# First FFN of a four-module kernel: the scan's preparation in single parts, two W_dt products to a pair of PSUM banks, light parts at the coming inputs' places

## Chip, cores and metric

The kernel runs on one core of a Trainium2 chip. The metric is the device time of one execution in microseconds (us), the median of several. A measurement of this kernel carries an uncertainty of about 0.2% (3.9 us).

## The reference, cut to what matters

The model is four modules in a row, each behind a layer norm and added to a residual stream x of four batches with 512 tokens and 512 channels: an attention, a first FFN with ternary weights, a selective scan (state space), and a block of latent attention with a mixture of experts. The change lies in the first FFN and in the preparation of the scan:

```python
# first FFN
h1 = jnp.einsum('bsd,hd->bsh', x, w1q)
h3 = jnp.einsum('bsd,hd->bsh', x, w3q)
g = jax.nn.silu(h1) * h3
return jnp.einsum('bsh,dh->bsd', g, w2q)
...
# scan
xz = jnp.einsum('btd,rd->btr', x, W_xproj)
delta_r, B_mat, C_mat = xz[..., :r], xz[..., r:r + n], xz[..., r + n:]
delta = jax.nn.softplus(jnp.einsum('btr,dr->btd', delta_r, W_dt) + b_dt)
dA = jnp.exp(delta[..., None] * A)
Bu = delta[..., None] * B_mat[:, :, None, :] * x[..., None]
h = dA_t * h + Bu_t            # over the tokens t
y = jnp.sum(h * C_t[:, None, :], axis=-1)
```

The hidden width of the FFN is 1365, that of the scan's state is 16, the rank of W_dt is 128. All is float32.

## The kernel before, in words

All four batches' x stay on the chip (xs, one tile each). The modules follow each other; TensorE's order is written by hand in all that matters here (`manual_schedule` for PE: the order of the Python calls is the order of TensorE's queue), while a planner orders the other engines' queues by its own costs. Every engine works through its queue in order.

**First FFN** (lines 676 to 718). The outer loop runs over the four batches b, the inner over eleven pieces f of the hidden width (ten of 128 rows, one of 85). `gated` (646) makes eight products with w1 and eight with w3 into the two halves of a pair of PSUM banks (pg; each product in two parts, high and low, for accuracy), ScalarE applies silu (658), VectorE multiplies by the other half (659, written to the tile sil), and the result is split into gh (ScalarE, 664) and gl (VectorE, 665). `down` (668) multiplies an earlier piece (the one before, for b > 0) by w2 into four single banks. PSUM has eight banks: two pairs (tag pair) and four single ones (tag bank). At the end of a batch VectorE adds the four banks to x (716).

Into this loop two generators are woven, each cut into parts by its yields. `part(n)` is called three times per piece, with n = 3f in the middle of `gated`, 3f+1 behind it, 3f+2 behind `down`: 33 places, n = 0 to 32.

- `inputs(b + 1)` (613), called `coming`: layer norm of the next batch and its transposes (tpf, 635), which ScalarE and VectorE read into hTh (640) and hTl (641). It gets the places n = 14, 17, 20, 23, 26, 29 and 32.
- `prepare(b - 1, ...)` (495), called `between`: all that the scan needs of the batch before. It gets the other places but 2, 3 and 5.

The parts of `prepare` before the change, in order: layer norm; two rows; four times a transpose into uT (131, 132); delta_r (pd, 522) in two parts; B and C (pb, 531) in two parts; B's transpose (pbt, 542); four parts with one W_dt product each (pz, 553), which ScalarE reads for |z + b| (Abs, 554) and VectorE for max(z + b, 0) (555); Exp over the whole tile (557); two parts with two u each (three VectorE operations per u, 561 to 563: the rounding of 1 + e is kept apart); Ln (566) with finish(0) and finish(1); and four parts turn_out(k), the first two with finish(k + 2). `finish` (569) adds Ln's result to delta (570), stores delta to HBM and multiplies it by uT (ux, 573). `turn_out` (575) transposes ux (tpd, 578), ScalarE copies it to the one buffer st (580), and a DMA stores it to dxs. These are 23 parts, and with the coming inputs there are 23 places for them: 0, 1, 4, 6 to 13, 15, 16, 18, 19, 21, 22, 24, 25, 27, 28, 30, 31. In the last pass (b = 3) nothing is coming, there are 30 places and the parts end at place 25.

Each part of `prepare` that needs TensorE takes a half of a pair of banks through `half_pair` (592), and the other half of that pair stays empty.

**Scan** (818 to 969). Eight single banks. For each batch, 16 states n and two halves, a step: ScalarE scales the rows bu (842) and makes da (848), TensorE transposes bu into two banks (856), VectorE scans them (864, 128x512, twice a step), GpSimd multiplies by C (hc, 875), TensorE adds hc up (888). The last batch's `prepare(3)` runs here, with banks of its own through `bank`: seven parts ahead of the steps, one part behind every second step from step 1 on. At step 6 of a batch (`fetch`, 829) the next one's delta_l and dxT, 1 MB each, are loaded; SP's queue issues these loads, the rows of C (cb, 872, one per two steps, into three buffers) and the stores of deltas and dxs. Behind the first batch's scan VectorE normalises it for the next module (`enter`, 107, 108, 738), into memory that held the tiles of `prepare(3)`.

The lines that call it:

```python
def part(n):
    if n % 3 == 2 and n > 3 * 4 and b + 1 < B:
        next(coming, None)
    elif n not in (2, 3, 5):
        next(between, None)
...
between = prepare(b - 1, bs, half_pair, 2) if b > 0 else iter(())
...
between = prepare(B - 1, cp, bank, 4)
```

Of the kernel before, what the change touches and what calls it, by code (L numbers as in the profile page):

```python
# [14 lines left out]
AF = mybir.ActivationFunctionType  # L15
ALU = mybir.AluOpType
# [3 lines left out]
P = 128  # L20
B, T, C = 4, 512, 512
NT = T // P
NK = C // P
# [23 lines left out]
def block_kernel(ctx: ExitStack, tc: tile.TileContext, a: dict, out: bass.AP):  # L47
    nc = tc.nc
# [15 lines left out]
    def pair(name):  # L64
        return banks["pair"].tile([P, 2, 512], F32, tag="pair", name=name)

    def bank(name):
        return banks["bank"].tile([P, 512], F32, tag="bank", name=name)
# [3 lines left out]
    def by_tokens(x, b):  # L72
        return x[b * T : (b + 1) * T, :].rearrange("(t p) c -> p t c", p=P)
# [53 lines left out]
    def transpose_into(dst, src, at, scale=1.0, spot=None):  # L127

        tp = (spot or bank)("tp")
        for k in range(NK):  # L130
            nc.tensor.transpose(tp[:, k * P : (k + 1) * P], src[:, k * P : (k + 1) * P], ident)  # L131
        nc.scalar.activation(  # L132
            dst[:, :, at : at + P], tp.rearrange("p (k q) -> p k q", k=NK), AF.Copy, scale=scale
        )
# [16 lines left out]
    with tc.tile_pool(name="a_w", bufs=1) as aw, tc.tile_pool(name="a_1", bufs=1) as a1, tc.tile_pool(  # L151
        name="a_2", bufs=2
# [234 lines left out]
        with tc.manual_schedule(engines={mybir.EngineType.PE}):  # L387
# [39 lines left out]
            for b in range(B):  # L427
                between = {m: [] for m in range(18)}
# [3 lines left out]
                if b + 1 < B:  # L432
                    n = b + 1
# [39 lines left out]
    wdt = sw.tile([P, C], F32, tag="wdt", name="wdt")  # L473
    nc.sync.dma_start(wdt, a["wdtT"])
    bdt = sw.tile([P, NK], F32, tag="bdt", name="bdt")
# [16 lines left out]
            nc.tensor.matmul(dp[:, k * P : (k + 1) * P], ones, diag, start=True, stop=True)  # L492
        nc.scalar.copy(dpar, dp)

    def prepare(b, pool, spot, ahead):


        x = xs[b]
        uT = pool.tile([P, NK, T], F32, tag="uT", name="uT")
        ops, rows = [], {}  # L500
        layer_norm(pool, x, lambda t, op: ops.append(op))
        yield

        def make(t):
            row = rows[t] = pool.tile([P, C], F32, tag="row", name="row_s", bufs=ahead)
            ops[t](row)
            ud = pool.tile([P, C], F32, tag="u", name="ud")
            nc.gpsimd.tensor_tensor(ud, row, dpar, ALU.mult)
            nc.gpsimd.tensor_tensor(x[:, t, :], x[:, t, :], ud, ALU.add)

        make(0)
        make(1)
        yield
        for t in range(NT):
            transpose_into(uT, rows.pop(t), t * P, spot=spot)
            if t == 1:
                make(2)
                make(3)
            yield
        pd = spot("pd")  # L520
        for k in range(NK):
            nc.tensor.matmul(pd, wx[:, k, :RANK], uT[:, k, :], start=k == 0, stop=k == NK - 1)
            if k == 1:
                yield
        drT = pool.tile([P, T], F32, tag="drT", name="drT")
        nc.scalar.copy(drT, pd)
        yield

        pb = spot("pb")
        for k in range(NK):  # L530
            nc.tensor.matmul(
                pb[: 2 * NS, :], wx[:, k, RANK:], uT[:, k, :], start=k == 0, stop=k == NK - 1
            )
            if k == 1:
                yield
        bcT = pool.tile([2 * NS, T], F32, tag="bcT", name="bcT")
        nc.scalar.copy(bcT, pb[: 2 * NS, :])
        nc.sync.dma_start(c_rows[b], bcT[NS:, :])
        yield
        pb = spot("pbt")  # L540
        for t in range(NT):
            nc.tensor.transpose(
                pb[:, t * NS : (t + 1) * NS], bcT[:NS, t * P : (t + 1) * P], ident[:NS, :NS]
            )
        nc.scalar.copy(bts[:, b, :], pb[:, : NT * NS])
        yield


        delta = pool.tile([P, NK, T], F32, tag="delta", name="delta")
        e = pool.tile([P, NK, T], F32, tag="e", name="e")  # L550
        for k in range(NK):
            pz = spot("pz")
            nc.tensor.matmul(pz, wdt[:, k * P : (k + 1) * P], drT, start=True, stop=True)
            nc.scalar.activation(e[:, k, :], pz, AF.Abs, bias=bdt[:, k : k + 1])
            nc.vector.tensor_scalar(delta[:, k, :], pz, bdt[:, k : k + 1], 0.0, ALU.add, ALU.max)
            yield
        nc.scalar.activation(e, e, AF.Exp, scale=-1.0)
        yield
        for k in range(NK):
            u = pool.tile([P, T], F32, tag="u", name="u")  # L560
            nc.vector.tensor_scalar(u, e[:, k, :], 1.0, -1.0, ALU.add, ALU.add)
            nc.vector.tensor_tensor(u, e[:, k, :], u, ALU.subtract)
            nc.vector.tensor_tensor(delta[:, k, :], delta[:, k, :], u, ALU.add)
            if k % 2 == 1:
                yield
        nc.scalar.activation(e, e, AF.Ln, bias=1.0)
        scaled = {}

        def finish(k):
            nc.vector.tensor_tensor(delta[:, k, :], delta[:, k, :], e[:, k, :], ALU.add)  # L570
            nc.sync.dma_start(deltas[b, k * P : (k + 1) * P, :], delta[:, k, :])
            scaled[k] = pool.tile([P, T], F32, tag="ux", name="ux", bufs=2)
            nc.vector.tensor_tensor(scaled[k], delta[:, k, :], uT[:, k, :], ALU.mult)

        def turn_out(k):
            tp, ux = spot("tpd"), scaled.pop(k)
            for t in range(NT):
                nc.tensor.transpose(tp[:, t * P : (t + 1) * P], ux[:, t * P : (t + 1) * P], ident)
            st = pool.tile([P, NT, P], F32, tag="st", name="st")
            nc.scalar.copy(st.rearrange("p t q -> p (t q)"), tp)  # L580
            nc.sync.dma_start(by_tokens(dxs, b)[:, :, k * P : (k + 1) * P], st)

        finish(0)
        finish(1)
        yield
        for k in range(NK):
            turn_out(k)
            if k + 2 < NK:
                finish(k + 2)
            yield  # L590

    def half_pair(name):
        return pair(name)[:, 0, :]


    with tc.tile_pool(name="b_s", bufs=1) as bs, tc.tile_pool(name="b_1", bufs=1) as b1, tc.tile_pool(
        name="b_2", bufs=2
# [78 lines left out]
        with tc.manual_schedule(engines={mybir.EngineType.PE}):  # L676
            for _ in inputs(0, first_mv):
                pass
            for f in range(3):
                quantize_down(f)  # L680
            for b in range(B):
                hT = high_low.pop(b)
                between = prepare(b - 1, bs, half_pair, 2) if b > 0 else iter(())
                coming = inputs(b + 1) if b + 1 < B else iter(())
                ys = None

                def part(n):  # L690
                    if n % 3 == 2 and n > 3 * 4 and b + 1 < B:
                        next(coming, None)
                    elif n not in (2, 3, 5):
                        next(between, None)


                lag = GBUFS - 1 if b == 0 else 1
                pending = []
                for f, rows in enumerate(FROWS):
                    pending.append((f, rows, gated(b, f, rows, hT, lambda: part(3 * f))))  # L700
                    if b == 0 and f + 3 < NF:
                        quantize_down(f + 3)
                    if b == 0 and f == 6:
                        clear()
                    part(3 * f + 1)
                    if b == 0 and f == 4:
                        scan_constants(b2)
                    if len(pending) > lag:
                        if ys is None:
                            ys = [bank(f"y{t}") for t in range(NT)]  # L710
                        down(b, *pending.pop(0), ys)
                    part(3 * f + 2)
                for job in pending:
                    down(b, *job, ys)
                for t in range(NT):
                    nc.vector.scalar_tensor_tensor(  # L716
                        xs[b][:, t, :], ys[t], scales["w2"][:, 2:3], xs[b][:, t, :], ALU.mult, ALU.add
                    )
# [100 lines left out]
    with tc.tile_pool(name="c_f", bufs=2, reuse_waits="tile") as cf, tc.tile_pool(  # L819
        name="c_1", bufs=1  # L820
# [76 lines left out]
        fetch(0)  # L897
        last = ExitStack()
        cp = last.enter_context(tc.tile_pool(name="c_p", bufs=1, side="right", reuse_waits="tile"))
        between = prepare(B - 1, cp, bank, 4)  # L900
        come = enter(0, c1)
        with tc.manual_schedule(engines={mybir.EngineType.PE}):
            for _ in range(2):
# [124 lines left out]
    with tc.tile_pool(name="d_1", bufs=1) as d1, tc.tile_pool(name="d_2", bufs=2) as d2, tc.tile_pool(  # L1028
        name="d_3", bufs=3
# [145 lines left out]
        with tc.manual_schedule(engines={mybir.EngineType.PE}):  # L1175
# [3 lines left out]
            n = len(pairs)  # L1179
            each = n // B  # L1180
            for m in range(n + 3):
                b, at = divmod(m, each)
# [35 lines left out]
    with tc.tile_pool(name="e_1", bufs=1, reuse_waits="tile") as e1, tc.tile_pool(  # L1218
        name="e_2", bufs=2, reuse_waits="tile"
# [127 lines left out]
        for c in range(2):  # L1347
# [19 lines left out]
            for n in range(TT):  # L1367
                nc.tensor.matmul(
                    found[:, : 2 * n_tiles], unit[:, n, :], what[:, n].rearrange("p s i -> p (s i)"),
                    start=n + c == 0, stop=n + c == TT,  # L1370
# [92 lines left out]
        for t in range(NT):  # L1463
            n = (B - 1) * NT + t
# [74 lines left out]
```

## Time and profile before

| | |
|---|---|
| median of three runs | 1933.17 us (1933.12 to 1936.76) |
| the profiled execution | 1941.33 us |
| its span, first to last instruction | 1939.6 us |
| mean granted TensorE clock | 0.967 |
| busy, share of the span: TensorE, VectorE, ScalarE, GpSimd | 91%, 59%, 49%, 30% |
| first FFN | 433 to 768 us |
| scan | from the first scan operation at 784 us to 1140 us |

The profile is one execution. Rows of a timeline give the start (us from the span's start), the duration (us), engine, line, operation, output <- inputs, shape, how many alike follow each other (xN), and in brackets the idle time of the engine just before with what ended it. A product in full float32 shows as two records. Rows of stages give busy time of each engine in a stretch, with the clock that TensorE was granted (1.00 is full). One execution lasts longer than the median of the unprofiled ones by 8.16 us.

### The profile page before, as it was taken

Reading aid. Unit: us, or ns where it says so; the run is one execution under the profiler, and the core shown is the slowest. Engines: PE = TensorE matmul, PEld = TensorE weight load, DVE = VectorE, ACT = ScalarE, POOL = GpSimd, SP = SyncE. Lnnn points to the kernel's source line nnn. Section 1 sums busy time; section 2 is a strip of 40 time slices with the busy share of each in tenths; the row PEclk is TensorE's granted clock in tenths of the full one; section 3 lists DMA queues with packets and bytes.
Section 4 is the critical chain, followed back from the end, with each engine's and each line's share of the span. In section 5 each row is a group of like instructions: output and inputs, shape, how many; then the busy total and the mean of one; then the engine's idle time right before and its main releaser. Section 6 shows DMA issues by size and latency. Waiting matters only on the chain. (4 is left out here: it accounts for less than half of the span.)

```text
span 1939.6 us, 26716 instructions
## 1 busy us (share of the span) xinstructions
PE 1764.7 (91%) x9970; PEld 1063.5 (55%) x9970; DVE 1143.7 (59%) x1849; ACT 946.0 (49%) x1945; POOL 580.8 (30%) x391
## 2 busy tenths in 40 slices
PE   7999999989999996977888788999999989999998
PEld 3433343437666664766776655555555554544544
DVE  6456435666454545898999985566574663422222
ACT  2433433332242434978999955556675662111111
POOL 2221212120202020966999850000001000144441
PEclk9999999999999998978999987999999999999999
DMA  7003200101000104115131100000001004645445
GB/s 246 8 1 94 75 1 1 44 25 53 1 34 12 44 1 146 40 60 168 53 101 53 50 14 1 1 1 23 1 23 33 23 2 145 223 88 92 87 83 140
DMA packets 67525, 111.09 MB, mean 57 GB/s; under 512 B 7627, under 2 KB 26443, under 8 KB 67349
## 3 DMA queue, kind: packets, MB, share of 16 engines
q1 hardware_dynamic: 58164, 88.02, 13.8%
q0 software_dynamic: 8656, 20.32, 5.8%
q8 instruction: 80, 1.31, 0.3%
q10 hardware_dynamic: 576, 1.05, 0.1%
q14 instruction: 49, 0.39, 0.1%
HBM read 81.18 MB, written 31.33 MB: 58 GB/s over the span
## 5 line engine op out<-in xcount | busy, mean ns | idle before, releaser
L875 POOL TENSOR_TENSOR hc<-h,cb 128x1024 f32<-128x1024 f32 x128 | 303.4, 2415 | 43.5 <-DVE h L864 28.9
L864 DVE TENSOR_TENSOR_SCAN h<-da,bu 128x512 f32<-128x512 f32 x256 | 289.5, 1197 | 19.4 <-ACT da L848 12.2
L856 PE MATMUL bu<-ident,bu 128*128 128x128 f32 x1024 | 163.7, 291 | 48.8 <-DVE h L864 25.0
L271 PE MATMUL pq<-wqkv,hT 128*128 128x512 f32 x384 | 180.9, 619 | 0.7 <-ACT hT L132 0.7
L842 ACT ACTIVATE bu<-dxT,bts 128x512 f32<-128x512 f32 x256 | 164.4, 721 | 4.6 <-DVE x L716 2.8
L856 PEld LDWEIGHTS bu<-ident,bu 128*128 128x128 f32 x1024 | 122.7, 148 | 79.9 <-ACT bu L842 42.9
L848 ACT ACTIVATE da<-delta_l,am 128x511 f32<-128x511 f32 x256 | 164.6, 721 | 3.6 <-DVE h L864 3.6
L1116 ACT ACTIVATE pr<-scd,nm 128x128 f32<-128x128 f32 (+3 forms) x256 | 132.9, 527 | 58.8 <-DVE nm L1113 56.0
L888 PE MATMUL ys<-ident,hc 128*128 128x128 f32 x1024 | 144.4, 286 | 16.0 <-POOL hc L875 14.0
L653 PE MATMUL pg<-hTh,w 128*128 128x512 f32 (+1 forms) x352 | 148.6, 422 | 4.1 <-DVE sil L659 2.9
L653 PE MATMUL pg<-hTl,w 128*128 128x512 f32 (+1 forms) x352 | 141.5, 402 | 0.2 <-DVE hTl L641 0.2
L1418 PE MATMUL pgr<-wgu,gTe 128*128 x304 | 137.1, 593 | 0.0
L888 PEld LDWEIGHTS ys<-ident,hc 128*128 128x128 f32 x1024 | 121.6, 148 | 26.7 <-POOL hc L875 23.4
L351 ACT ACTIVATE pt<-sc 128x1024 f32<-128x1024 f32 (+3 forms) x128 | 84.1, 697 | 84.2 <-PE sc L346 81.7
L271 PEld LDWEIGHTS pq<-wqkv,hT 128*128 128x128 f32 x384 | 72.0, 196 | 94.7 <-issue 86.2
L1105 PE MATMUL scd<-qkTd 32*128 32x512 f32 (+3 forms) x512 | 108.3, 504 | 12.9 <-ACT pr L1116 11.9
L102 POOL TENSOR_TENSOR ri_ln<-ri_ln,minus_half 128x4 f32<-128x4 f32 (+1 forms) x17 | 16.9, 993 | 319.0 <-DVE ri_ln L101 314.5
L1113 DVE TENSOR_REDUCE nm<-scd 128x2 f32<-128x256 f32 (+3 forms) x128 | 104.0, 813 | 0.0
L1128 PEld LDWEIGHTS tpd<-ident,pr 128*128 128x128 f32 x640 | 70.5, 145 | 60.9 <-issue 41.2
L1128 PE MATMUL tpd<-ident,pr 128*128 128x128 f32 x640 | 102.3, 292 | 0.6 <-ACT pr L1116 0.6
L352 POOL TENSOR_SCALAR_AFFINE_SELECT pt<-pt 128x512 f32<-128x512 f32 x64 | 43.1, 674 | 196.7 <-ACT pt L351 196.7
L1108 DVE TENSOR_TENSOR scd<-scd,neg 128x256 f32<-128x256 f32 x128 | 54.7, 428 | 66.7 <-PE scd L1105 64.9
(263 smaller groups left out, 3107.8 us busy)
## 6 DMA issues: line engine op xcount, KB each, us to landing
cb<-c_rows SPq DMA_DIRECT2D x64, 256.0 KB, 3.1
q_w<-in_w2T SPq DMA_DIRECT2D x20, 256.0 KB, 2.9
deltas<-delta SPq DMA_DIRECT2D x16, 256.0 KB, 2.6
dxs<-st SPq DMA_DIRECT2D x16, 256.0 KB, 2.3
delta_l<-deltas SPq DMA_DIRECT2D x4, 1024.0 KB, 9.5
dxT<-dxs SPq DMA_DIRECT2D x4, 1024.0 KB, 7.1
hrows<-h SPq DMA_DIRECT2D x4, 1024.0 KB, 5.4
acc<-x SPq DMA_DIRECT2D x16, 256.0 KB, 2.0
```

The source lines that it names most:

```text
L271: nc.tensor.matmul(y, inputs_T[b][:, k, t * P : (t + 1) * P], wqkv[:, k, s * C : (s + 1) * C], start=k == 0, stop=k == NK - 1,)
L653: nc.tensor.matmul(pg[:rows, i, :], w[:, k, f * P : f * P + rows], part[:, k, :], start=k + m == 0, stop=k + m == NK,)
L842: nc.scalar.activation(row, dxT[:, t, :], AF.Copy, scale=bts[:, b, t * NS + n : t * NS + n + 1])
L848: nc.scalar.activation(da[:, k, 1:], delta[:, k, 1:], AF.Exp, scale=am[:, k, n : n + 1])
L856: nc.tensor.transpose(bu[i][:, t * P : (t + 1) * P], scaled[b, n][t][:, k * P : (k + 1) * P], ident)
L864: nc.vector.tensor_tensor_scan(h[:, i, :], decays[b, n][:, 2 * half + i, :], bu, 0.0, ALU.mult, ALU.add)
L875: nc.gpsimd.tensor_tensor(hc, states.pop((b, n, half)), weighed[b, n].unsqueeze(1).to_broadcast([P, 2, T]), ALU.mult)
L888: nc.tensor.matmul(sums[b][t][:, k * P : (k + 1) * P], hc[:, i, t * P : (t + 1) * P], ident, is_transpose=True, start=n == 0 and k == 0, s ...
L1105: nc.tensor.matmul(sc[:, i, :w], qkT[at, g, t * P : w], qkT[at, NG + g, :w], start=True, stop=True)
L1116: nc.scalar.activation(pr[:, i, :w], sc[:, i, :w], AF.Exp, bias=nm[:, i : i + 1], accum_out=sums[b, g][:, t, 2 * p + i : 2 * p + i + 1],)
L1128: nc.tensor.transpose(tp[:, j * P : (j + 1) * P], pr[:, i, j * P : (j + 1) * P], ident)
L1418: nc.tensor.matmul(pg, gT[:, k, :], wgu[:, bass.ds(e, 1), k, :].rearrange("p e o -> p (e o)"), start=k == 0, stop=k == NK - 1,)
```

## The change

It touches `prepare`, the function that hands out PSUM, and `part`; the arithmetic stays the same.

- `prepare` gets a second argument for PSUM, `spots`, which gives two spots at once: in the FFN the two halves of one pair of banks (`halves`), in the scan two single banks. The four W_dt products are made two by two, in two parts in place of four.
- The parts behind them are cut smaller: each u is a part, Ln is a part, finish(0) and finish(1) are parts, and each finish(k + 2) is a part behind its turn_out. `prepare` has 27 parts in place of 23.
- A yield tells whether the coming part needs no TensorE (True: Exp, u, Ln, finish). At a place that goes to the coming inputs, `part` lets such a light part go along.

The parts' places in the passes b = 1 and 2 are then: W_dt products at 15 and 16, Exp at 17, u at 18 to 21, Ln at 22, finish(0) and finish(1) at 23 and 24, turn_out at 25, 27, 30 and 31, finish(2) and finish(3) at 26 and 28. In b = 3: W_dt products at 14 and 15, Exp 16, u 17 to 20, Ln 21, finish 22 and 23, turn_out 24, 26, 28 and 29. In the scan the W_dt products come behind the steps 9 and 11 (before: 9, 11, 13, 15) and the turn_outs behind the steps 29, 33, 37 and 39 (before: 25, 27, 29, 31).

```diff
-    def prepare(b, pool, spot, ahead):
+    def prepare(b, pool, spot, spots, ahead):
...
-        for k in range(NK):
-            pz = spot("pz")
-            nc.tensor.matmul(pz, wdt[:, k * P : (k + 1) * P], drT, start=True, stop=True)
-            nc.scalar.activation(e[:, k, :], pz, AF.Abs, bias=bdt[:, k : k + 1])
-            nc.vector.tensor_scalar(delta[:, k, :], pz, bdt[:, k : k + 1], 0.0, ALU.add, ALU.max)
-            yield
+        for half in range(2):
+            for i, pz in enumerate(spots("pz")):
+                k = 2 * half + i
+                nc.tensor.matmul(pz, wdt[:, k * P : (k + 1) * P], drT, start=True, stop=True)
+                nc.scalar.activation(e[:, k, :], pz, AF.Abs, bias=bdt[:, k : k + 1])
+                nc.vector.tensor_scalar(delta[:, k, :], pz, bdt[:, k : k + 1], 0.0, ALU.add, ALU.max)
+            yield half == 1
         nc.scalar.activation(e, e, AF.Exp, scale=-1.0)
-        yield
+        yield True
         for k in range(NK):
...
-            if k % 2 == 1:
-                yield
+            yield True
         nc.scalar.activation(e, e, AF.Ln, bias=1.0)
+        yield True
...
         finish(0)
+        yield True
         finish(1)
         yield
         for k in range(NK):
             turn_out(k)
             if k + 2 < NK:
+                yield True
                 finish(k + 2)
             yield
...
+    def halves(name):
+        both = pair(name)
+        return both[:, 0, :], both[:, 1, :]
...
-                between = prepare(b - 1, bs, half_pair, 2) if b > 0 else iter(())
+                between = prepare(b - 1, bs, half_pair, halves, 2) if b > 0 else iter(())
...
+                light = [False]
                 def part(n):
                     if n % 3 == 2 and n > 3 * 4 and b + 1 < B:
                         next(coming, None)
-                    elif n not in (2, 3, 5):
-                        next(between, None)
+                        if not light[0]:
+                            return
+                    if n not in (2, 3, 5):
+                        light[0] = next(between, False)
...
-        between = prepare(B - 1, cp, bank, 4)
+        between = prepare(B - 1, cp, bank, lambda name: (bank(name), bank(name)), 4)
```

## The prediction

> **What bounds the kernel now.** I read the share of busy time first (TensorE 91% over the span), then the busy time by stage, then each engine's timeline around the changed code, with the idle time in front of each instruction. In the first FFN (433 to 768 us) the stage rows show TensorE busy 63.1 of 70 us in pass b=1, 82.2 of 88 in b=2, 79.3 of 92 in b=3: TensorE sets the stage's end and only its idle time can be won. TensorE's timeline names the large holes. The first row below is a gated product, the other three are turn_out's first transpose in the passes b=1, 2, 3:
>
> ```profile
> 559.43 0.50 PE L653 MATMUL pg<-hTh,w 128*128 128x512 f32 x1 [1.38 <-DVE sil L659]
> ...
> 570.72 0.63 PE L578 MATMUL tpd<-ident,ux 128*128 128x128 f32 x4 [3.15 <-DVE hTl L641]
> ...
> 661.33 1.12 PE L578 MATMUL tpd<-ident,ux 128*128 128x128 f32 x4 [3.06 <-DVE hTl L641]
> ...
> 742.97 1.09 PE L578 MATMUL tpd<-ident,ux 128*128 128x128 f32 x4 [9.13 <-DVE ux L573]
> ```
>
> The transposes wait because Ln, finish(0) and finish(1) stand directly before them and VectorE's queue is full. After each of them the granted clock is halved; after the 1.38 us it isn't. Busy time by window (us; PE, PEld, DVE, ACT, POOL, then clock):
>
> ```profile
> 557.92:561.34 3.42, 2.04 (x10) 1.59 (x9) 3.39 (x7) 1.21 (x2) 0.00 (x0) 1.00 0.00 0
> 571.58:575.00 3.42, 3.42 (x12) 2.68 (x11) 1.39 (x3) 0.87 (x2) 0.00 (x0) 0.50 0.59 211
> 660.33:667.16 6.83, 5.83 (x18) 4.86 (x19) 3.76 (x7) 1.80 (x2) 0.00 (x0) 0.50 0.44 159
> 738.84:745.66 6.82, 2.69 (x9) 2.34 (x10) 4.30 (x7) 2.63 (x3) 0.00 (x0) 0.50 0.31 115
> ```
>
> One W_dt product with its two readers is the row from which the new wait is priced (TensorE, ScalarE, VectorE):
>
> ```profile
> 538.70 1.02 PE L553 MATMUL pz<-drT,wdt 128*128 128x512 f32 x2
> 539.15 0.80 PE L653 MATMUL pg<-hTh,w 128*128 128x512 f32 x1
> ```
> ```profile
> 539.76 0.69 ACT L554 ACTIVATE e<-pz,bdt 128x512 f32<-128x512 f32 x1 [2.93 <-PE pz L553]
> ```
> ```profile
> 540.48 0.75 DVE L555 TENSOR_SCALAR delta<-pz,bdt 128x512 f32<-128x512 f32 x1 [2.93 <-ACT e L554]
> ```
>
> In the scan, prepare(3) runs beside b=0. VectorE is busy 108.4 of 116 us there; its two holes, and one preparation operation that waits for GpSimd to finish an hc (0.69 us elsewhere), are:
>
> ```profile
> 833.33 2.75 DVE L562 TENSOR_TENSOR u<-e,u 128x512 f32<-128x512 f32 x1
> ...
> 892.41 2.33 DVE L864 TENSOR_TENSOR_SCAN h<-da,bu 128x512 f32<-128x512 f32 x2 [5.75 <-ACT da L848]
> ```
> ```profile
> 914.45 1.00 DVE L738 TENSOR_SCALAR h<-x,mv_d,ri_ln 128x512 f32<-128x512 f32 x2 [3.27 <-POOL ri_ln L102]
> ```
>
> **The change, part by part.** The number of instructions stays the same on every engine, and behind the scan the order is the same: all is decided between 538 and about 930 us. The sum is made against the profiled execution, 1941.33 us (span 1939.6); the median of the runs is 1933.17, and I carry the difference over.
>
> *1. What goes.* Exp, the four u parts, Ln and finish(0), finish(1) now come at places 17 to 24 in b=1 and 2 and the first turn_out at 25, where Ln and finish stood at 25 and turn_out at 27 before; the last turn_out keeps its place (31). So the waits ahead of the transposes go, with the half clock behind them. b=1: 1.38 + 3.15, and 1.8 for the half clock (the block of eight gated products took 3.14 us from 571.10 instead of 1.86, transposes and first products some 0.5 more). b=2: 1.38 + 3.06, half clock 2.9 (same way). b=3: 9.13, half clock 1.35 (half of the 2.69 us of work in the window). Sum 6.3 + 7.3 + 10.5 = 24.1 us.
>
> *2. What comes: a wait inside a pair.* In the built program both halves are one tile, and the second W_dt product waits on VectorE: by the semaphore count, for the max of the first half, which waits for its Abs. TensorE's order is written by hand, so the gated products behind it wait too. Price: the first product occupies TensorE 0.86 us (538.70 to 539.79, where the gated products come at their steady 0.23 again, less 0.23). Abs starts 1.06 us after the product, max ends at 541.23 (540.48 + 0.75), and TensorE resumes some 0.07 us later (559.37 to 559.43 elsewhere). 541.30 - 539.56 = 1.74 us idle. Two pairs in each of three passes: 6 x 1.74 = 10.4 us. From below it could be 0, if the wait were covered; but only gated products stand behind, on the same queue. From above, with an Abs or a max (0.69, 0.75) ahead of it, 2.5 each. I take 1.74. Between the pairs eight gated products (1.86 us) cover the second half's readers.
>
> *3. What is late next.* I walk the changed order with these durations (Abs 0.69, table load 1.28, Exp and Ln 1.92, a u part 1.8, max or product with sil 0.75, gl, hTl, ux 0.68). In b=1 and 2 VectorE does u0 and u1 (3.7 us) before the sil product of f=6, so gated 7 waits 0.84; then 0.37 (gated 8), 0.65 (turn_out 0 for ux), 0.83 and 0.38 (turn_out 1 and 2 for hTl): 3.1 each, and up to 0.4 at the end, where st still waits for its predecessor's DMA. In b=3 two table loads and Exp stand ahead of f=5's sil, and u1 ahead of its gl: the down products wait 1.8; turn_out 0 waits 1.08 for f=7's sil product.
>
> b=1: 3.5 + 3.1 + 0.3 - 6.3 = +0.6. b=2: 3.5 + 3.1 + 0.4 - 7.3 = -0.3. b=3: 3.5 + 2.9 - 10.5 = -4.1. **FFN: -4** (-14 without the pair's wait, +6 with waits of 2.5 and a us of each new stall mis-sized).
>
> *4. Half clock behind the new waits.* Between windows with 1.38 us idle (full clock next) and gaps of 3.06 (half clock) nothing in the FFN tells; 1.74 is nearer to 1.38, so I take nothing; the upper end is 2.9 us each, from b=2. The Trainium skill ("TensorE: Matmul & The Clock Gate", Part 1) gives an idle window of about 3.4 us as what halves the clock: by it these waits cost nothing more, but the trace halves it after 3.06 already.
>
> *5. The scan.* There the pair is two banks, two tiles, so no wait within it; the next turn must wait for the scan before it, and VectorE has the two max (1.3 us) to do meanwhile: nothing. The Ln stands where it stood, but u is done earlier. The turn_outs move from steps 25, 27, 29, 31 to 29, 33, 37, 39. That takes st's DMA out of the way of the 1 MB loads of delta_l and dxT, behind which the last one landed late: the 5.75 us go. The 3.27 stay in another form: the next normalisation writes where prepare's tiles lay and waits for all stores of dxs, whose last is now 4 steps (10 us) later; I take 3 again, ends 0 and 6. Against it, u and ux stand apart from each other more, and each start beside an hc may wait the 2.06 of the row above (2.75 - 0.69): one more, ends 0 and 3. Sum -5.75 + 2.06 = **-3.5** (-9 to +4).
>
> Sum: -4 - 3.5 = -7.5: 1933.8 for the profiled execution, **1925.7** for the median.
>
> **Rivals.**
> - *Slower: the half clock.* Each of the six waits is followed by two half-clock windows, as the 3.06 us were: 6 x 2.9 = 17.4, less 7.5: +9.9, **1943**. It decides if a window with about 1.7 us idle counts as idle. For it: 585 to 589 us, where two small gaps (2.03 together) were enough for one window. Against it: 1.38, and that one window each (1.8) would only give +3.3.
> - *No change: the scan gives it back.* The store of st comes last now, VectorE waits for it 6 us, two operations more wait for GpSimd (4.1): scan +4.4, FFN -4: **1933.5**, or up to some us below. For it: VectorE works in order, and the long rows above.
> - *Much faster: the pair's wait doesn't bind.* Without 10.4 us the sum is -17.9: **1915.3**. Only the built order speaks against it. The Trainium skill ("PSUM — Partial Sum Buffer", PSUM bank collisions) keeps engines apart by bank, and the halves are two banks: by it no wait is needed; no run here has shown one.
> - *It doesn't do what it says*: the preparation still ends at place 31, so a part shifted early wins only what the transposes waited; this is in the forecast.
>
> **How the numbers follow.** A measurement of this kernel tells about 0.2% (3.9 us) from no change: 1929.3 to 1937.0. Forecast 0.46 (1921 to 1930), no change 0.24, half clock 0.18, no wait 0.12. Faster: 0.46 + 0.12 = 0.58; same 0.24; slower 0.18. The range leaves out the far parts of the half-clock and the no-wait cases: 1917 to 1941.
>
> **What would show it.** Right: TensorE idle 1.7 us ahead of each second W_dt product in the FFN, released by the max; no wait over 1.2 us at turn_out's first transpose in b=1, 2, 3; the down products of f=5 in b=3 waiting for gl. In the scan: st no longer waiting for its DMA and no 5 us hole before the scans of n=17. Wrong: clock 0.5 right behind the W_dt pairs, a hole of over 5 us at the first normalisation behind b=0's scan, or no idle time within a pair.

## The result, and the profile after

The changed kernel takes 1923.79 us (median of four runs, 1921.02 to 1926.95) beside 1933.97 us for the kernel before (median of four, 1933.12 to 1936.76). The ratio is 0.9945 with a 95% interval of 0.9925 to 0.9966, so it is faster by 0.3 to 0.75%, some 10.6 us of 1935. The forecast was -7.5 us. The profiled execution took 1926.95 us with a span of 1925.2 us, 14.4 us less than that of before. One of the six executions of the kernel e8 below was a slow one of 3411.99 us; it counts in the median given for e8 (1915.92 us, without it 1914.78), but not in its ratio.

TensorE's timeline of the changed kernel, at the places that the prediction spoke of: the two W_dt products of the first pair in b=1, the gated product behind it, and turn_out's first transposes in b=1, 2 and 3.

```profile
540.10 1.02 PE L554 MATMUL pz<-drT,wdt 128*128 128x512 f32 x2
...
542.68 1.12 PE L554 MATMUL pz<-drT,wdt 128*128 128x512 f32 x2 [1.56 <-DVE delta L556]
...
557.80 0.50 PE L660 MATMUL pg<-hTh,w 128*128 128x512 f32 x1 [0.72 <-DVE sil L666]
...
568.43 0.63 PE L579 MATMUL tpd<-ident,ux 128*128 128x128 f32 x4 [0.61 <-DVE ux L574]
...
654.93 0.63 PE L579 MATMUL tpd<-ident,ux 128*128 128x128 f32 x4 [0.61 <-DVE ux L574]
...
738.33 0.66 PE L579 MATMUL tpd<-ident,ux 128*128 128x128 f32 x4 [1.28 <-DVE sil L666]
```

The waits of 3.15, 3.06 and 9.13 us are now 0.61, 0.61 and 1.28; the last is a little over the 1.2 us that the prediction had set as its sign of being right. The new wait stands inside the pair, released by the max (delta). The table of TensorE's waits from 520 to 765 us gives its sum (us in all, times, longest):

```profile
PE pz L554 <- DVE delta L556: 9.4, 6, 1.6
...
PE pg L660 <- DVE sil L666: 1.4, 2, 0.7
PE tpd L579 <- DVE sil L666: 1.3, 1, 1.3
PE tpd L579 <- DVE ux L574: 1.2, 2, 0.6
```

The clock stays full behind the pair and behind the transposes (busy time by window, columns as before; the clock is the 1.00):

```profile
542.80:546.20 3.40, 3.40 (x12) 2.02 (x12) 0.75 (x1) 1.11 (x2) 0.00 (x0) 1.00 0.00 0
...
570.10:573.50 3.40, 3.40 (x19) 2.52 (x18) 3.40 (x6) 1.45 (x3) 0.00 (x0) 1.00 0.78 268
...
656.60:660.00 3.40, 3.40 (x19) 2.52 (x18) 3.05 (x5) 1.45 (x3) 0.00 (x0) 1.00 0.70 242
```

In the scan, VectorE's timeline has no hole of 5.75 us any more. Its cause stood on ScalarE in the kernel before, which had to wait for the store of st before it could copy the next block into it, with bu and da behind:

```profile
888.67 0.58 ACT L580 COPY st<-tpd 128x512 f32<-128x512 f32 x1 [5.00 <-DMA dxs<-st]
```

In the changed kernel the four copies there wait 0.3 us for the store in all. The hole at the first normalisation is still there, and a u operation beside an hc still takes 2.75 us:

```profile
814.87 2.75 DVE L563 TENSOR_TENSOR u<-e,u 128x512 f32<-128x512 f32 x1
...
903.70 1.00 DVE L749 TENSOR_SCALAR h<-x,mv_d,ri_ln 128x512 f32<-128x512 f32 x2 [3.88 <-ACT da L859]
```

By stage, from one x<-y to the next in the FFN, and from the first scan operation to the 225th of 256 (the middle of the last batch):

| us | b=1 | b=2 | b=3 | three passes | scan, 224 operations |
|---|---|---|---|---|---|
| before | 89.25 | 89.36 | 90.21 | 268.8 | 312.3 |
| after | 87.64 | 84.83 | 84.51 | 257.0 | 306.4 |

So this execution won 11.8 us in the FFN where -4 was forecast, and 5.9 us in the scan where -3.5 was forecast. That is 17.7 us, and the span is 14.4 us shorter: the rest of this execution, whose code is as before, took 3.3 us longer.

The scan also shows what the new wait hangs on. The code there has the same order (product, Abs, max, then the second product), but its pair is two single tiles. TensorE makes both products without a wait, as four records in one row:

```profile
797.84 1.88 PE L554 MATMUL pz<-drT,wdt 128*128 128x512 f32 x4
```

In the FFN the two halves are two banks as well, but one tile, and there the second product waits 1.56 us.

### The profile page after: what moved, and what is told of

Read it like the earlier page. It is cut to its first block, busy times and chain, and to the rows that moved or that the text cites. A ratio compares the mean times of both kernels' runs of the same rounds, so it can differ in the third digit from the quotient of the medians.

```text
span 1925.2 us, 26704 instructions
## 1 busy us (share of the span) xinstructions
PE 1756.5 (91%) x9970; PEld 1054.1 (55%) x9970; DVE 1143.7 (59%) x1849; ACT 947.5 (49%) x1945; POOL 581.2 (30%) x391
## 3 DMA queue, kind: packets, MB, share of 16 engines
q10 hardware_dynamic: 576, 1.05, 0.1%
## 5 line engine op out<-in xcount | busy, mean ns | idle before, releaser
L660 PE MATMUL pg<-hTh,w 128*128 128x512 f32 (+1 forms) x352 | 144.7, 411 | 2.4 <-DVE sil L666 1.7
```

The lines of the kernel that those rows point to most:

```text
L660: nc.tensor.matmul(pg[:rows, i, :], w[:, k, f * P : f * P + rows], part[:, k, :], start=k + m == 0, stop=k + m == NK,)
```

## The experiments

All edits are on the changed kernel unless something else is said. Ratios are to the kernel before, run on the same chip; 0.001 is 1.9 us. The kernels of a group (e1 to e4, e5 to e8, e9 and e10) share their runs of the kernel before; across groups, and with the changed kernel's first runs, they are compared by their ratios.

**e1 and e2: each half alone.** In e1 the scan's `prepare(3)` is the function of before (`prepare_old`). e2 is an edit on the kernel before: only the scan's `prepare(3)` is the changed function (`prepare_new`), and the FFN stays as it was.

```diff
# e1, on the changed kernel
-between = prepare(B - 1, cp, bank, lambda name: (bank(name), bank(name)), 4)
+between = prepare_old(B - 1, cp, bank, 4)
# e2, on the kernel before
-between = prepare(B - 1, cp, bank, 4)
+between = prepare_new(B - 1, cp, bank, lambda name: (bank(name), bank(name)), 4)
```

> The FFN keeps the changed preparation, the scan gets the preparation of before. Theory: the two halves of the change add up. The profiled execution after is 11.8 us ahead of before at the end of the FFN, so this kernel gains some 8 us by the median (6 to 12; 1924 to 1928), its FFN passes last 87.7, 84.8 and 84.5 us, and the 5.75 us hole of VectorE and the 3.3 us one in the scan of batch 0 are back. Rival: the scan's holes come from when the FFN ends and not from the places of the turn_outs; then this kernel is as fast as the changed one (within 2 us) and has no 5 us hole.

> The reverse: the FFN of before, the changed preparation in the scan. Theory: 4 us faster than before by the median (2 to 6; 1928 to 1932), the 5.75 us hole ahead of the scans of n=17 gone, a hole of 3 to 4 us ahead of the first normalisation. Rival: the scan gives nothing of its own: within 1.5 us of before.

e1: 1931.4 us, ratio 0.9970 (0.9959 to 0.9980), -5.8 us. e2: 1930.96 us, 0.9974 (0.9961 to 0.9986), -5.0 us. Their sum, -10.8, agrees with the whole, -10.6. The theory of two gains that add up holds, though the FFN's is just below what was expected (6 to 12), and its pass b=2 lasted 87.8 us and not 84.8. VectorE's holes go with the preparation of the scan and not with the FFN's end. e1 has the two of before:

```profile
882.34 2.33 DVE L972 TENSOR_TENSOR_SCAN h<-da,bu 128x512 f32<-128x512 f32 x2 [5.60 <-ACT da L956]
...
904.39 1.00 DVE L846 TENSOR_SCALAR h<-x,mv_d,ri_ln 128x512 f32<-128x512 f32 x2 [3.29 <-POOL ri_ln L102]
```

e2 has only the second, and here the profile names its releaser, the store of st:

```profile
913.25 1.00 DVE L838 TENSOR_SCALAR h<-x,mv_d,ri_ln 128x512 f32<-128x512 f32 x2 [4.04 <-DMA dxs<-st]
```

**e3: pairs only.** The FFN of before with the W_dt products in pairs, and everything behind them in the parts and at the places' rule of before; the scan of before. It is an edit on the kernel before.

```diff
-for k in range(NK):
-    pz = spot("pz")
+for half in range(2):
+    for i, pz in enumerate(spots("pz")):
+        k = 2 * half + i
...
     yield
```

> In the FFN two W_dt products to a pair of banks, but the parts of before behind them (two u each, Ln with finish(0) and finish(1) ahead of the first turn_out) and no light parts at the coming inputs' places; the scan is that of before. Theory: the gain comes from the single parts, the pairs cost. The six waits of 1.57 us are there, the first turn_out still waits (3 us in b=1 and 2, 8 to 9 in b=3) with the half clock behind it: 5 to 10 us slower than before (1938 to 1944). Rival: the pairs win, by putting every later part two places earlier; then it is 4 or more us faster than before.

1942.81 us, ratio 1.0034 (1.0021 to 1.0048): 6.6 us slower than before, as the theory said. The pairs' waits came and the transposes' stayed (TensorE's waits, 520 to 772 us):

```profile
PE pz L554 <- DVE delta L556: 9.4, 6, 1.6
PE tpd L579 <- DVE ux L574: 7.3, 1, 7.3
PE tpd L579 <- DVE hTl L743: 6.2, 2, 3.1
```

Against e1 (same FFN but for the parts, same scan) the single parts with their places are worth 12.4 us, from 1.0034 to 0.9970. The pairs by themselves cost. What they give is two places fewer, which by a count of the places the larger number of single parts needs to fit into the pass; no run had single parts without pairs.

**e4: the products ahead of their readers.**

```diff
-for i, pz in enumerate(spots("pz")):
+pair_z = spots("pz")
+for i, pz in enumerate(pair_z):
     k = 2 * half + i
     nc.tensor.matmul(pz, wdt[:, k * P : (k + 1) * P], drT, start=True, stop=True)
+for i, pz in enumerate(pair_z):
+    k = 2 * half + i
     nc.scalar.activation(e[:, k, :], pz, AF.Abs, bias=bdt[:, k : k + 1])
```

> The changed kernel, but both W_dt products of a pair are issued ahead of the four instructions that read them. Theory: the 9.4 us of idle time within the pairs go; the readers now start behind the second product, so the second pair waits some 0.6 us in each pass: 7.5 us faster than the changed kernel (5 to 9; 1915 to 1919). Rival: the wait only moves, since VectorE and ScalarE get no earlier and the next gated products need what they read: within 2 us of the changed kernel.

1927.6 us, ratio 0.9956 (0.9942 to 0.9969): 2.1 us slower than the changed kernel by the ratios, which their intervals do not tell from none. The rival was right. TensorE's waits from 520 to 765 us show where the saving went:

```profile
PE tpd L582 <- DVE ux L577: 6.8, 3, 2.4
...
PE pz L555 <- DVE delta L559: 3.6, 3, 1.2
```

The pairs' waits fell from 9.4 to 3.6 us, and the first turn_outs' rose from 2.5 to 6.8 (2.19, 2.19 and 2.39). TensorE reaches the transposes earlier, and ux is no earlier: the line W_dt, Exp, u, Ln, ux on ScalarE and VectorE runs from the products to the first turn_out, and it was only 0.6 to 1.3 us longer than the time that TensorE took to get there.

**e5: a longer wait inside the pair.** The max of each pair's first half is done twice in the FFN (the second writes the same values).

```diff
+if ahead == 2 and i == 0:
+    nc.vector.tensor_scalar(delta[:, k, :], pz, bdt[:, k : k + 1], 0.0, ALU.add, ALU.max)
```

> The changed kernel with the max of each pair's first half done twice in the FFN, so that the wait within a pair lasts one more VectorE operation (0.75 us): six waits of 2.3 us in place of 1.57. Theory: the clock is decided in fixed stretches of 3.41 us, and a stretch with about 1.8 us idle or more puts the next one at half clock (1.68 us idle left it at full, 1.99 us halved it in the traces so far). A gap of 2.3 us lies with 1.8 us or more in one stretch in some 60% of the places on that grid: three to five of the six are followed by half clock, 1.7 us each, so 4.5 + 5 to 8 = 9 to 13 us slower than the changed kernel. Rival: the clock falls only where nearly a whole stretch is idle: no half clock behind the pairs, 4.5 us slower.

1933.06 us, ratio 0.9985 (0.9970 to 0.9999): 7.8 us slower than the changed kernel, between the two expectations. Four waits were 2.35 us, two 2.82. Only one of the six was followed by half clock, not three to five. The windows of the clock's own grid say why:

```profile
539.45:542.87 3.42, 1.42 (x5) 0.50 (x3) 1.21 (x2) 0.69 (x1) 0.00 (x0) 1.00 0.00 0
542.87:546.28 3.41, 3.06 (x5) 1.84 (x6) 0.52 (x2) 0.69 (x1) 0.00 (x0) 0.50 0.00 0
...
635.02:638.43 3.41, 1.59 (x5) 1.03 (x6) 1.50 (x2) 0.62 (x2) 0.00 (x0) 1.00 0.00 0
638.43:641.84 3.41, 2.26 (x8) 1.10 (x7) 1.90 (x3) 2.04 (x4) 0.00 (x0) 1.00 0.00 0
```

A window with 2.00 us idle (3.42 less 1.42 busy) put the next at 0.50; one with 1.82 idle left it at 1.00. The other waits lay across a border of the grid, with 1.7 us or less on each side. The theory of a fixed grid holds; my count of how many gaps it would catch was wrong. A wait of 1.57 us never halved the clock in any run.

**e6: the last store from another queue.**

```diff
-nc.sync.dma_start(by_tokens(dxs, b)[:, :, k * P : (k + 1) * P], st)
+queue = nc.scalar if ahead == 4 and k == NK - 1 else nc.sync
+queue.dma_start(by_tokens(dxs, b)[:, :, k * P : (k + 1) * P], st)
```

> The changed kernel, but the last store of dxs in the scan's preparation is issued from ScalarE's queue and not from SP's, where it stands behind the next row of C. Theory: the 3.9 us hole ahead of the first normalisation behind batch 0 is the wait for this store (st is written at 895.5 us, the store is issued at 898.0 and lands some 4 us behind that): it is issued 2.5 us earlier, the hole shrinks to 1 to 1.5 us and the kernel is 2 to 3 us faster than the changed one. Rival: the normalisation waits for ri_ln from GpSimd or for something else: the hole stays between 3 and 4 us and the time within 1 us.

1922.67 us, ratio 0.9929 (0.9910 to 0.9949). In the changed kernel SP's queue shows the store right behind the row of C, 2.5 us after st was written (895.5 us):

```profile
897.62 0.32 SPq L883 DMA_DIRECT2D cb<-c_rows  x1
898.03 0.39 SPq L582 DMA_DIRECT2D dxs<-st  x1
```

In e6 the normalisation follows the scan without a hole (no bracket):

```profile
899.88 4.56 DVE L876 TENSOR_TENSOR_SCAN h<-da,bu 128x512 f32<-128x512 f32 x4
904.35 4.12 DVE L750 TENSOR_SCALAR h<-x,mv_d,ri_ln 128x512 f32<-128x512 f32 x2
```

The hole was the wait for the store: theory right on the cause (the row of the changed kernel, 3.88 us, names ScalarE's da; with the store issued earlier the hole is gone). The scan's 224 operations took 304.0 us instead of 306.4, which is 2.4 us of the 3.88 of the hole. About 0.9 us of what is missing stands in the normalisations: the first two, now beside an hc, take 4.12 us in place of 1.00, and the next two 1.04 in place of 3.26. The difference of 3 us by the ratios is within the two intervals.

**e7: one place earlier.** The preparation also gets place 5, and an empty part holds the first turn_out where it was.

```diff
-    if n not in (2, 3, 5):
+    if n not in (2, 3):
...
         finish(1)
         yield
+        if ahead == 2:
+            yield
```

> The changed kernel; in the FFN the preparation also gets place 5, so its parts stand one place earlier, and an empty part stands ahead of the first turn_out, which keeps its place. The products of a pair are ordered as in the changed kernel. Theory: the line from the W_dt products over Exp, u, Ln and ux is what the first turn_out waits for; with one place more (2.7 us) the waits of 0.61, 0.61 and 1.28 us at its first transpose go, the six waits of 1.57 us stay: 2 to 3 us faster than the changed kernel. Rival: VectorE is behind everywhere and the waits only change their place: within 1 us.

1936.59 us, ratio 1.0002 (0.9989 to 1.0014): 11 us slower than the changed kernel, which neither expectation had. The transposes in b=1 and 2 no longer wait, as the theory said. But Ln, with a table load on either side, now stands ahead of silu in ScalarE's queue:

```profile
560.24 1.28 ACT L566 ACT_TABLE_LOAD   x1 [2.47 <-DVE u L563]
561.53 1.92 ACT L566 ACTIVATE e<-e 128x2048 f32<-128x2048 f32 x1
563.47 1.28 ACT L667 ACT_TABLE_LOAD   x1
564.76 0.69 ACT L667 ACTIVATE sil<-pg,sc_w 128x512 f32<-128x512 f32 x1
```

The gated products wait 3.15 and 3.11 us for sil (1.4 us in all in the changed kernel), and half clock is back behind both. The three passes took 268.2 us. In the changed kernel Ln stands behind that silu. The order on ScalarE is the planner's; that this order alone makes the 11 us was not tried apart.

**e8: e4 and e7 together.**

> Both: the products of a pair ahead of their readers, and the preparation one place earlier with an empty part ahead of the first turn_out. Theory: with the products first alone, 5.8 of the 9.4 us of the pairs' waits were saved but 4.3 came back as waits of the first turn_out for ux; with one place more these have no cause, and the second pair comes two places behind the first: pair waits under 1 us in all, turn_out waits under 1 us each, 7 to 10 us faster than the changed kernel (1914 to 1917). Rival: what is saved ahead of the readers always comes back at the next thing that VectorE makes: within 2 us of the changed kernel.

1915.92 us, ratio 0.9895 (0.9871 to 0.9919): 9.6 us faster than the changed kernel, as the theory said, though neither edit gains alone. TensorE's waits from 512 to 757 us:

```profile
PE pg L665 <- DVE sil L671: 2.3, 2, 1.1
...
PE tpd L582 <- DVE hTl L653: 1.4, 2, 0.7
PE tpd L582 <- DVE sil L671: 1.1, 1, 1.1
```

No row names pz, and TensorE's timeline has no gap of 0.25 us or more ahead of a W_dt product. With the products first the planner leaves Ln behind silu (ScalarE: silu at 557.34, Ln's table load at 558.04), so e7's loss does not come.

**e9 and e10: all three edits, and the changed kernel once more.**

> The three edits together on the changed kernel: products of a pair ahead of their readers, preparation one place earlier with an empty part ahead of the first turn_out, and the last store of dxs from ScalarE's queue. Theory: the gain of the FFN (some 9 us against the changed kernel) and that of the scan (the hole of 3.6 us ahead of the first normalisation gone) are independent and add up: 12 us faster than the changed kernel, ratio to before 0.987 to 0.989. Rival: with the FFN shorter the store is no longer what the normalisation waits for, and the time is that of the two FFN edits alone (0.9895) within 1 us.

> The changed kernel once more, unedited, beside the kernel with three edits on the same chip, with a second profile. Theory: the code of its FFN gave passes of 84.8 us (b=2) in one execution and 87.3 to 87.8 in two others, by where the fixed stretches of the clock fell; the three passes last 257 to 262 us in all, and the ratio to before is 0.9935 to 0.9955. Rival: the first profile shows what this kernel always does: b=2 lasts 84.8 us again, with no half clock in the FFN.

e9: 1914.59 us, ratio 0.9894 (0.9874 to 0.9915). It is the fastest kernel here but not told apart from e8: by the time the rival is right. By the trace the hole ahead of the normalisation is gone and the scan takes 304.0 us instead of e8's 306.2; its FFN took 251.9 us instead of 249.9, with 3.4 us more of half clock at the start of b=2. Whether the store's 2 us are kept in the median stays open.

e10: 1924.48 us, ratio 0.9944 (0.9928 to 0.9960), the same as the first time. Its passes (busy time by window, then the clock):

```profile
499.43:587.86 88.43, 80.46 (x341) 57.35 (x340) 45.91 (x72) 33.69 (x47) 12.66 (x9) 0.99 0.08 25
587.86:675.29 87.43, 82.65 (x341) 59.12 (x341) 45.41 (x69) 33.70 (x47) 12.95 (x9) 0.97 0.08 25
675.29:759.71 84.42, 78.34 (x325) 55.56 (x324) 41.64 (x63) 31.59 (x43) 12.96 (x9) 1.00 0.12 40
```

b=2 took 87.4 us, not 84.8: the theory holds. The same FFN code took 257.0, 259.7 (e1), 261.5 (e6) and 260.3 us (e10), the code of before 268.8 and 268.3 (e2). The means are 259.6 and 268.6, so the FFN's gain is 9.0 us, and 2.8 of the 11.8 in the first profile were the luck of one execution, mostly of where the clock's grid fell.

## Why the prediction was right, point by point

The sign, the likeliest case and the range held; the two parts of the forecast, -4 and -3.5, were each too small in the traces (-9.0 and -5.9). The terms of the FFN, against the first profile (the half clock's trace value is the difference of TensorE's busy time, 243.65 us before and 238.64 after):

| term | forecast, us | trace, us |
|---|---|---|
| 1: waits that go (1.38 and 3.15; 1.38 and 3.06; 9.13) | -18.1 | -18.1 |
| 1: half clock behind them | -6.0 | -5.0 (e1, e6, e10: -1.9 to -2.2) |
| 2: waits inside the pairs | +10.4 | +9.4 |
| 3: what is late next | +9.8 | +5.0 |
| small holes at the passes' ends and starts | not counted | -3.1 |
| sum | -4 | -11.8 |

*1. What goes* was right: every wait named is gone, and the half clock behind it. The half clock that a run keeps behind the end of b=1 (586.67 to 593.5 us in e10) was not in the terms.

*2. The wait inside a pair* was right, in its cause, its releaser and its size: 1.56 us each where 1.74 was worked out. So "the pair's wait doesn't bind" is out for the kernel as it is. But its price was not its length: e4 took away 5.8 us of it and gained nothing that can be measured. The wait overlaps with the line of ScalarE and VectorE that the first turn_out needs anyway; the 9.4 us can only be won together with one place more for this line (e8, -9.6). The case "without 10.4 us the sum is -17.9" therefore counted a saving that by itself comes back, as e4 shows. The Trainium skill ("PSUM — Partial Sum Buffer", PSUM bank collisions), which the prediction cites, finds no need for a wait between two banks. The built program keeps it for the tile that holds both halves: in the scan, where the pair is two tiles, the same order of code makes no wait. Two tiles in the FFN were not tried.

*3. What is late next* is the step that was mis-sized: 5.0 us in place of 9.8. Gated 7 waited 0.72 (0.84 worked out) and the first turn_outs 0.61, 0.61 and 1.28 (0.65, 0.65, 1.08), so these were close. The waits of gated 8 (0.37) and of turn_out 1 and 2 for hTl (0.83 and 0.38) did not come, and the down products of f=5 in b=3 waited 1.1 (0.32 and 0.78) in place of 1.8. In the walk each whole u part went ahead of what stood behind it; VectorE's queue puts hTl and gl between the first and the second of the three operations of u2 (557.66 u, 557.99 hTl, 558.60 gl, 559.19 u). The two holes of 1.05 us in which y waited for gl at the start of b=2 and b=3 went too, which the walk, beginning at the W_dt products, could not see.

*4. No half clock behind the new waits* was right, and the slower rival is out: no window behind any of the 1.57 us waits was halved. The prediction chose the nearer of two values, 1.38 and 3.06 us, and in so far this was luck. Read by the clock's stretches of 3.413 us, the trace of before says more: 1.58 us idle left the next stretch full (732.01 to 735.42 us), 2.06 us halved it (656.92 to 660.33 us). The border can now be drawn in as 1.8 to 2.0 us within one stretch (e5, e2). Even waits of 2.35 and 2.82 us (e5) brought half clock behind one of six and 7.8 us in all, so the rival's 1943 would have needed still longer ones.

*5. The scan.* The 5.75 us went and the hole ahead of the normalisation stayed, 3.88 us where 3 was taken, for the reason given: the last store of dxs (e2 names it, e6 removes it). The "one more" wait for GpSimd did not come: six operations of the preparation are long in both kernels (after: 2.75, 2.75, 2.74, 4.24 for two, and 1.34), and they cost 9.8 us above their usual lengths, as much as before. Without the +2.06 the step would have given -5.6, and -5.9 was measured. (The step's terms as written add up to -3.7, not -3.5.) "The scan gives it back" is out: e2 gains 5.0 us.

*What stays open.* The stages give -9.0 and -5.9, the comparisons of whole runs -5.8 (e1), -5.0 (e2) and -10.6 (whole). The scan's agree; of the FFN's gain about 3 us are missing in the whole runs. What lies outside the three passes and the 224 scan operations took between 853 and 864 us in the twelve profiled executions (858.5 before, 861.8 after, 855.4 in e10), without following the edits, so one profile of each kernel can't place them. Executions of one kernel scatter by 5 us or more (e1: 1927.15 to 1933.16).

## What to carry to other kernels

A wait that a trace shows is worth its length only if the next thing in the queue was ready; before taking one away, follow the line of the other engines from its cause to the next place where they meet, and shorten or shift that line in the same edit (e4 and e7 gain nothing or lose, together they gain 0.5%). Work shifted in single parts pays where it lets short, urgent operations in between; but any part with a table load has to be followed on ScalarE's queue, since a planner may put it ahead of what TensorE waits for. A gain of some microseconds in a stage should be read from two or three executions, since the same FFN code took 257.0 to 261.5 us here.

## What the runs showed of the hardware

The granted clock changes only at the borders of stretches of 3.413 us. In the middle of the FFN's passes, from full clock, the next stretch was halved when about 2.0 us or more of one stretch were idle (1.99 in e2); 1.82 us left it full (e5). The Trainium skill ("TensorE: Matmul & The Clock Gate", Part 1) tells of a window of 3413 ns that runs freely; the trace agrees with 3.413 us. It says that the half clock comes after an idle window of that length; here 2.00 idle of 3.42 was enough, and the measurement decides. Behind the end of pass b=1, 1.40 to 1.44 us of idle time were enough in four executions (before, e1, e2, e7), but 1.62 us left the clock full in the changed kernel's first profile (582.9 to 586.3 us). The products behind that end use 85 of 128 rows. They fill all of the 2.0 us of busy time of that stretch in the kernel before, and 0.07 us of it in the changed one. It may be that such work counts as less than busy. Counted by its rows it would leave 2.1 us idle before and 1.65 after (an estimate), on the two sides of the border above; e1, with 1.70 us by that count, was halved and does not fit, and this was not tried. In the scan, among 128x128 transposes, the idle time alone does not decide: 1.35 us was enough once (e2, at 820.5 to 823.9 us), and 1.95 us left the clock full (e10, at 835.8 to 839.3 us).

A VectorE operation on two tensors that starts beside a GpSimd hc took up to 2.75 us instead of 0.69, in every kernel here. In the six long operations of the changed kernel's preparation it ended 0.55 us behind the end of the hc that was running: 2.75 us with 2.2 us of the hc left, 1.34 with 0.8 left. A hole of VectorE that is closed in the scan can so give back less than its length: of 3.9 us 2.4 were kept in e6.
